# An attention and feed-forward kernel: turned tokens loaded from the host, means and deviations spread by way of DRAM

## The chip, the cores and the metric

The kernel runs on one core of one Trainium2 chip. A core has five engines with an instruction stream each: TensorE (PE in the profile; its weight loads are PEld), VectorE (DVE), ScalarE (ACT), GpSimd (POOL) and SyncE (SP), which here only issues DMAs. Engines run their own stream in order and wait for each other through semaphores. The metric is the device time of one execution in microseconds, as a median over runs.

## The reference

There are 8 sequences of 256 tokens with 256 features, all float32. Attention uses the normalized tokens as queries and the given context as both keys and values; then a gated feed-forward network with ternary weights follows, each part with a residual.

```python
def _layernorm(x, axis=-1, eps=1e-05):
    m = jnp.mean(x, axis=axis, keepdims=True)
    v = jnp.var(x, axis=axis, keepdims=True)
    return (x - m) / jnp.sqrt(v + eps)
...
        scores = jnp.einsum('bqd,bkd->bqk', query, key) * scale          # scale = 1/16
        scores = jnp.where(causal[None, :, :], neg_inf, scores)
        scores = jnp.where(key_pad, neg_inf, scores)
        attn = jax.nn.softmax(scores, axis=-1)
        out = jnp.einsum('bqk,bkd->bqd', attn, value)
...
        h = jax.nn.silu(_tlin(x, w1_w, w1_s)) * _tlin(x, w2_w, w2_s)      # 256 -> 1024
        h = jax.nn.gelu(_tlin(h, h1_w, h1_s), approximate=False)          # 1024 -> 1024
        h = jax.nn.gelu(_tlin(h, h2_w, h2_s), approximate=False)          # 1024 -> 1024
        return _tlin(h, w3_w, w3_s)                                       # 1024 -> 256
    x = x + _L0_xattn_ref(_layernorm(x, axis=-1), ctx_1024, ctx_1024, mask_BxS2_ik1)
    x = x + _L0_ffn_ref(_layernorm(x, axis=-1), ...)
```

## The kernel before

The 2048 tokens are cut into four blocks of 512 tokens (two sequences, four tiles of 128 tokens each). Attention works with tokens on the partitions, the feed-forward network with features on the partitions and the 512 tokens of a block along the free axis. So a tile of tokens has to be turned with TensorE transposes (`turned`, line 202) twice in a block before: the normalized tokens `ya` into `pqt` and from there into the queries `qt`, and the normalized tokens after attention `yf` into `pyt`, from there into the two parts `hyt` and `lyt`. The residual `xs` is turned too, into `pxt` and `xst`.

Matrix products of the feed-forward network run in a fast float32 form on a high part and a low part of the activations: ACT writes the high part, DVE subtracts it to get the low part (`rest`, line 214), and TensorE multiplies both (`layer`, line 379). Since only the weights' lower bits could make that inexact, the kernel also checks the weights: `look_through` loads pieces of the weights again into two buffers `raw` (SP, line 166), DVE reduces each to a column of `seen` (`look`, line 158), and a second, exact network, which is not run with these inputs, stands behind a branch on the outcome. Weights themselves come in by POOL's queue (line 117).

The order of work is the order in which the program is written: each engine's stream is the order of emission. `feed_forward(t)` is a generator with 26 steps: steps 0 to 7 are the gated first layer, 8 to 15 the layer `h1`, 16 to 23 the layer `h2`, 24 and 25 the output `po`. Attention for block t+1 is another generator, `stages`, and is emitted a piece at a time between the steps of block t: its pieces stand behind steps 8, 9, 11, 12, 13, 15, 17, 18, 19, 20 and 22 (`STAGES`). A load for the weight check and a look at the one before it stand behind each of the steps 8 to 20 (`LOOKS`), after the piece of attention if the step has one:

```python
            if n in STAGES:
                next(ahead, None)
            if n in LOOKS:
                next(looking, None)
```

The pieces before are, in order: statistics of `xs` (step 8), normalization to `ya` (9), the mask's bias on POOL and the transposes to `pqt` with their copies to `qt` (11), the scores `ps` and their maxima (12), exponentials (13), transposes of the probabilities (15), the product with the values and the residual (17), statistics again (18), normalization to `yf` (19), `pxt` and `xst` (20), `pyt` and its two parts (22). Block 0's attention has no earlier block to hide behind; it runs first, in two halves of one sequence each, before any feed-forward step. At the start of block t's steps the inputs of block t+1 are loaded by SP: `xs`, the mask `mi` broadcast to all partitions, the turned context `kt`, the context `vs`.

All buffers named here have one copy, except `raw`, `xst`, the hidden layers (two) and the temporary `tmp` (four), from which a step's second gelu `g` is taken.

Of the kernel before, what the change touches and what calls it, by code (L numbers as in the profile page):

```python
# [23 lines left out]
F32 = mybir.dt.float32  # L24
# [6 lines left out]
P = 128  # L31
# [28 lines left out]
def _network(ctx, tc, g, exact, flag):  # L60
# [10 lines left out]
    work = pool("work", 1)  # L71
    hp = pool("hidden", 1)
    ps_at = pool("ps_at", 4, space=bass.MemoryType.PSUM)
    ps_mm = pool("ps_mm", 4, space=bass.MemoryType.PSUM)
# [14 lines left out]
    def load_block(t):  # L89
        xs = new(io, [P, NT, D], "xs", f"xs_{t}")  # L90
        kt = new(io, [P, ND, TB], "kt", f"kt_{t}")
        vs = new(io, [P, NT, D], "vs", f"vs_{t}")
        mi = new(io, [P, TB], "mi", f"mi_{t}", I32)
        rows = bass.ts(t, TB)
        step = NT if t else 1
        for i in range(0, NT, step):
            own = bass.ds(t * TB + i * P, step * P)
            nc.sync.dma_start(  # L98
                out=xs[:, i : i + step, :], in_=g.x[own, :].rearrange("(i p) d -> p i d", p=P)
            )  # L100
        nc.sync.dma_start(out=mi, in_=g.mask[:, rows].to_broadcast([P, TB]))
        for js in groups(t):
            own = bass.ds(t * TB + js[0] * S, len(js) * S)
            nc.sync.dma_start(
                out=kt[:, :, tokens(js)],
                in_=g.ctx_t[:, own].rearrange("(c p) k -> p c k", p=P),
            )
        nc.sync.dma_start(out=vs, in_=g.ctx_n[rows, :].rearrange("(i p) d -> p i d", p=P))
        return xs, kt, vs, mi
# [29 lines left out]
    eps = new(const, [P, 1], "eps", "eps")  # L139
    nc.gpsimd.memset(eps, EPS)  # L140

    junk = new(const, [P, 1], "junk", "junk")
# [98 lines left out]

    def stages(t, js, once, result, xs, kt, vs, mi):
        cols = tokens(js)
# [5 lines left out]
        yield  # L249
        bias = once("bias", "bias", [P, NB, SW])  # L250
        for j in js:
            k0, k1 = (mi[:, j * S + k * P : j * S + (k + 1) * P] for k in range(2))
            parts = [bias[:, j, k * P : (k + 1) * P] for k in range(3)]
            nc.gpsimd.tensor_scalar(parts[1], k0, 0.0, NEG, ALU.is_equal, ALU.mult)  # L254
            nc.gpsimd.tensor_tensor(parts[0], parts[1], causal, ALU.add)
            nc.gpsimd.tensor_scalar(parts[2], k1, 0.0, NEG, ALU.is_equal, ALU.mult)
            nc.gpsimd.tensor_tensor(parts[2], parts[2], causal, ALU.add)
        qt = once("qt", "qt", [P, ND, TB])
        for n, (c, pt) in enumerate(turned(y, js, f"pqt_{t}_{js[0]}")):

            if n % 2 == 0:
                nc.scalar.activation(qt[:, c, cols], pt, AF.Copy, scale=1.0 / 16.0)
            else:
                nc.vector.tensor_scalar(qt[:, c, cols], pt, 1.0 / 16.0, None, ALU.mult)
        table(t, js, AF.Exp)
        yield
        s = once("y", "s", [P, NB, SW])
        nmax = once("nmax", "nmax", [P, NB, 2])
        for j in js:
            ps = ps_at.tile([P, TB], F32, tag="at", name=f"{v}ps_{t}_{j}")  # L270
            for h, (a, e) in enumerate(SPANS):
                for c in range(ND):
                    nc.tensor.matmul(  # L273
                        ps[:, a:e],
                        lhsT=qt[:, c, bass.ts(2 * j + h, P)],
                        rhs=kt[:, c, bass.ds(j * S, e - a)],
                        start=(c == 0),
                        stop=(c == ND - 1),
                    )
            nc.vector.tensor_tensor(s[:, j, :], ps[:, :SW], bias[:, j, :], ALU.add)  # L280
            for h, (a, e) in enumerate(SPANS):
                nc.vector.tensor_reduce(
                    nmax[:, j, h : h + 1], s[:, j, a:e], AX.X, ALU.max, negate=True
                )
# [56 lines left out]
        yield  # L341
        y = once("y", "yf", [P, NT, D])
        normed(xs, js, mvf, y, f"f_{t}_{js[0]}")
        table(t, js, AF.Silu)
        yield
        xst = once("xst", "xst", [P, ND, TB], bufs=2)
        pxt = turned(xs, js, f"pxt_{t}_{js[0]}")
        if t:
            for c, pt in pxt:
                nc.scalar.copy(xst[:, c, cols], pt)  # L350
        elif js == groups(t)[-1]:
            keep_warm(WARM_LATER)
        yield
# [3 lines left out]
        for c, pt in turned(y, js, f"pyt_{t}_{js[0]}"):  # L357
            nc.scalar.copy(yt[0][:, c, cols], pt)  # L358
            if not exact:
                rest(yt[1][:, c, cols], pt, yt[0][:, c, cols])  # L360
        if not t:
            yield
# [91 lines left out]

    STAGES = (8, 9, 11, 12, 13, 15, 17, 18, 19, 20, 22)
    LOOKS = range(NH, NH + 13)
# [79 lines left out]
```

## Time and profile before

| | us |
|---|---|
| median of 3 runs (384.49 to 386.74) | 385.27 |
| the profiled execution | 383.81 |
| its span | 381.9 |
| PE busy | 371.5 |
| ACT busy | 179.9 |
| DVE busy | 175.1 |
| POOL busy | 36.2 |

The granted TensorE clock was 0.997 over the span. Busy time counts the instructions of an engine; weight loads overlap matmuls. The lines of the profile name the line of the kernel, the engine, the operation and the tiles (out<-in, numbers left out). The chain that ended last is followed back from the last instruction, at each step to what released it, or to the instruction before it on its engine. DMA times run from issue to landing; the DMA queue of SP is called SPq. In the lists by time, a count behind an x merges neighbouring instructions, and square brackets give the idle time before and what ended it.

### The profile page before, as it was taken

The numbers are of one execution on the slowest core, as the hardware profiler recorded it, in microseconds if no ns is written. First come the engines' busy times: TensorE is split into PE (matmuls) and PEld (weight loads), VectorE is DVE, ScalarE is ACT, GpSimd is POOL, SyncE is SP. The second block draws the span as 40 slices with busy tenths as digits, with TensorE's granted clock in tenths as the row PEclk, the third lists the DMA queues.
The fourth block names the chain that finished last, engine by engine and source line by source line (L and its number), as shares of the span: only waits on it lengthen the run. The fifth ranks groups of instructions, "written<-read, shape, count | busy, mean of one in ns | idle before, by whom it ended". The sixth has DMA issues, their size and how long they took to land.

```text
span 381.9 us, 4362 instructions
## 1 busy us (share of the span) xinstructions
PE 371.5 (97%) x1660; PEld 297.8 (78%) x1661; DVE 175.1 (46%) x360; ACT 179.9 (47%) x291; POOL 36.2 (9%) x70
## 2 busy tenths in 40 slices
PE   8799999999999999999999999999999999999994
PEld 4468888888888888888888888888888888888783
DVE  4757454347226575245424755434722643322111
ACT  4466644537335562833553664443633653323320
POOL 4732260000003100000000500000000000000000
PEclk9999999999999999999999999999999999999998
DMA  6799940211008011220105303121100101110001
GB/s 194 239 399 394 383 127 30 82 57 42 13 30 247 3 56 53 57 79 32 55 0 159 118 2 108 35 80 55 49 7 37 47 0 41 30 41 0 0 2 62
DMA packets 18763, 32.87 MB, mean 86 GB/s; under 512 B 1968, under 2 KB 8880, under 8 KB 18736
## 3 DMA queue, kind: packets, MB, share of 16 engines
q1 hardware_dynamic: 14560, 20.86, 17.7%
q0 software_dynamic: 4032, 11.54, 8.6%
q8 instruction: 15, 0.25, 0.2%
q10 hardware_dynamic: 144, 0.13, 0.1%
q14 instruction: 12, 0.10, 0.1%
HBM read 30.43 MB, written 2.10 MB: 85 GB/s over the span
## 4 chain that ended last, share of the span: by engine, by line
PE 93%; DVE 1%; POOL 1%; ACT 1%; DMA 1%; SPq 0%; issue 0%
PE pm L379 63%; PE pa L379 8%; PE po L379 8%; PE pb L379 8%; PE pv L321 2%; PE ps L273 2%; DMA mi<-mask 1%; PE pxt L202 1%; PE pyt L202 1%; PE pqt L202 1%; PE pp L303 1%; SPq L98 0%; DVE xs L329 0%; DVE stf L179 0%; POOL bias L254 0%
## 5 line engine op out<-in xcount | busy, mean ns | idle before, releaser
L214 DVE TENSOR_TENSOR lh<-g,hh 128x512 fp32r<-128x512 f32 x64 | 44.5, 695 | 148.8 <-ACT g L423 148.8
L420 ACT ACTIVATE hh<-pm,sc 128x512 fp32r<-128x512 f32 x64 | 44.1, 688 | 138.2 <-PE pm L379 138.1
L379 PE MATMUL pm<-hh,h 128*128 128x512 f32 x256 | 66.3, 401 | 0.0
L379 PE MATMUL pm<-hha,h 128*128 128x512 f32 x256 | 65.7, 399 | 0.0
L379 PE MATMUL pm<-lh,h 128*128 128x512 f32 x256 | 64.9, 395 | 0.0
L379 PE MATMUL pm<-lha,h 128*128 128x512 f32 x256 | 64.9, 395 | 0.0
L379 PEld LDWEIGHTS pm<-lh,h 128*128 128x128 f32 x256 | 48.1, 188 | 11.6
L379 PEld LDWEIGHTS pm<-lha,h 128*128 128x128 f32 x256 | 48.1, 188 | 11.6
L379 PEld LDWEIGHTS pm<-hha,h 128*128 128x128 f32 x256 | 47.9, 188 | 11.2
L379 PEld LDWEIGHTS pm<-hh,h 128*128 128x128 f32 x256 | 47.4, 188 | 10.6
L423 ACT ACTIVATE g<-pm,sc 128x512 f32<-128x512 f32 x64 | 43.6, 681 | 0.0
L403 ACT ACTIVATE gate<-pa,sc 128x512 f32<-128x512 f32 x32 | 22.0, 688 | 39.2 <-PE pa L379 39.2
L406 DVE SCALAR_TENSOR_TENSOR gate<-pb,sc,gate 128x512 f32<-128x512 f32 x32 | 24.0, 750 | 21.7 <-PE pb L379 16.8
L158 DVE TENSOR_REDUCE seen<-raw 128x1 f32<-128x512 uint16 (+1 forms) x48 | 30.2, 629 | 0.0
L214 DVE TENSOR_TENSOR lha<-gate,hha 128x512 fp32r<-128x512 f32 x32 | 22.4, 699 | 0.4
L379 PE MATMUL pa<-hyt,w 128*128 128x512 f32 x64 | 20.2, 397 | 0.7 <-ACT hyt L358 0.7
L254 POOL TENSOR_SCALAR bias<-mi 128x128 f32<-128x128 int32 x8 | 6.0, 748 | 154.8 <-DMA mi<-mask 154.4
L397 ACT CAST hha<-gate 128x512 fp32r<-128x512 f32 x32 | 19.6, 611 | 2.1 <-DVE gate L406 2.1
L379 PE MATMUL pa<-lyt,w 128*128 128x512 f32 x64 | 20.2, 397 | 0.0
L379 PE MATMUL pb<-hyt,w 128*128 128x512 f32 x64 | 20.1, 396 | 0.0
L379 PE MATMUL pb<-lyt,w 128*128 128x512 f32 x64 | 20.1, 396 | 0.0
L420 ACT ACT_TABLE_LOAD x13 | 16.7, 1283 | 0.2
(78 smaller groups left out, 329.2 us busy)
## 6 DMA issues: line engine op xcount, KB each, us to landing
h<-h1t POOLq DMA_DIRECT2D x8, 512.0 KB, 10.7
h<-h2t POOLq DMA_DIRECT2D x8, 512.0 KB, 14.7
raw<-h1t SPq DMA_DIRECT2D x16, 256.0 KB, 2.6
raw<-h2t SPq DMA_DIRECT2D x16, 256.0 KB, 2.6
vs<-ctx_n SPq DMA_DIRECT2D x4, 512.0 KB, 7.0
out<-o SPq DMA_DIRECT2D x7, 256.0 KB, 2.6
xs<-x SPq DMA_DIRECT2D x3, 512.0 KB, 5.3
kt<-ctx_t SPq DMA_DIRECT2D x3, 512.0 KB, 6.4
```

The source lines that it names most:

```text
L158: nc.vector.tensor_reduce(seen[:, n : n + 1], halves16[:, :, 0], AX.X, ALU.max)
L202: nc.tensor.transpose(pt[:, c, bass.ts(n, P)], y[:, i, bass.ts(c0 + c, P)], ident)
L214: nc.vector.tensor_tensor(lo, value, hi.bitcast(F32), ALU.subtract)
L254: nc.gpsimd.tensor_scalar(parts[1], k0, 0.0, NEG, ALU.is_equal, ALU.mult)
L273: nc.tensor.matmul(ps[:, a:e], lhsT=qt[:, c, bass.ts(2 * j + h, P)], rhs=kt[:, c, bass.ds(j * S, e - a)], start=(c == 0), stop=(c == ND - 1),)
L321: nc.tensor.matmul(pv[:, h, :], lhsT=prt[:, j, bass.ds(a + k * P, P)], rhs=vs[:, 2 * j + k, :], start=(k == 0), stop=(k == n - 1),)
L379: nc.tensor.matmul(pm, lhsT=wc[:, bass.ts(o, P)], rhs=x, start=(n == 0), stop=(n == len(steps) - 1),)
L397: nc.scalar.copy(hid[0][:, o, :], value)
L403: nc.scalar.activation(gate, pa, AF.Silu, scale=sc[:, 0, o : o + 1])
L406: nc.vector.scalar_tensor_tensor(values[o], pb, sc[:, 1, o : o + 1], gate, ALU.mult, ALU.mult)
L420: nc.scalar.activation(nxt[0][:, o, :], pm, AF.Gelu, scale=scale)
L423: nc.scalar.activation(value, pm, AF.Gelu, scale=scale)
```

## The change

For the blocks 1 to 3, the queries and the input of the feed-forward network are no longer turned on TensorE.

- The host passes a further array, `xt`, the turned tokens. `queries_loaded` loads a block of it into `qt`. The statistics are computed as before; the means go to all partitions through DRAM (`on_all`: a write of four values per partition, then a read that broadcasts the row of 512), DVE subtracts the row from `qt`, and the factor one over sixteen times the deviation is applied later, to the scores (`factor`, in one operation with the bias).
- For the feed-forward network, mean and reciprocal deviation both go through DRAM (two writes, two broadcast reads). `xst`, which is still turned on TensorE, less the mean (DVE) times the reciprocal deviation (POOL) gives `yf` in turned form. The two parts are taken from it a step later, behind step 23, which is new in `STAGES`.
- The rows land in a new tile `row` and, for the reciprocal deviations, in the mask's tile `mi`.
- In block 0 the four compare operations of the mask move from POOL to DVE; the additions stay on POOL.
- The space for POOL's DMA descriptors is set to 8192 bytes.

```diff
+    rows = pool("rows", 2, space=bass.MemoryType.DRAM)
...
-    def stages(t, js, once, result, xs, kt, vs, mi):
+    def mask_bias(t, js, once, mi):
+        bias = once("bias", "bias", [P, NB, SW])
+        engine = nc.gpsimd if t else nc.vector
+        for j in js:
+            k0, k1 = (mi[:, j * S + k * P : j * S + (k + 1) * P] for k in range(2))
+            parts = [bias[:, j, k * P : (k + 1) * P] for k in range(3)]
+            engine.tensor_scalar(parts[1], k0, 0.0, NEG, ALU.is_equal, ALU.mult)
+            nc.gpsimd.tensor_tensor(parts[0], parts[1], causal, ALU.add)
+            engine.tensor_scalar(parts[2], k1, 0.0, NEG, ALU.is_equal, ALU.mult)
+            nc.gpsimd.tensor_tensor(parts[2], parts[2], causal, ALU.add)
+        return bias
+
+    def on_all(values, tags, name):
+
+        n = values.shape[2]
+        there = new(rows, [n, NT, P], f"{len(tags)}", f"{name}")
+        for i in range(n):
+            nc.sync.dma_start(out=there[i].rearrange("i p -> p i"), in_=values[:, :, i])
+        got = []
+        for i, (p, tag, dt) in enumerate(tags):
+            row = new(p, [P, TB], tag, f"{name}{i}", dt).bitcast(F32)
+            nc.sync.dma_start(
+                out=row, in_=there[i : i + 1].rearrange("o i p -> o (i p)").to_broadcast([P, TB])
+            )
+            got.append(row)
+        return got
...
+    def queries_loaded(t, js, once, xs, mi):
+        qt = once("qt", "qt", [P, ND, TB])
+        nc.sync.dma_start(
+            out=qt, in_=g.xt[:, bass.ts(t, TB)].rearrange("(c p) q -> p c q", p=P)
+        )
+        mva = once("mva", "mva", [P, NT, nc.vector.BN_AGGR_DIM])
+        sums(xs, js, mva, f"a_{t}")
+        (mean,) = on_all(mva[:, :, 0:1], ((work, "row", F32),), f"ma_{t}")
+        yield
+        bias = mask_bias(t, js, once, mi)
+
+        std = once("sq", "sda", [P, NT])
+        nc.scalar.activation(std, mva[:, :, 1], AF.Sqrt, bias=eps256, scale=256.0)
+        rstd = once("rstd16", "rstd", [P, NT])
+        nc.vector.reciprocal(rstd, std)
+        yield
+        for c in range(ND):
+            nc.vector.tensor_tensor(qt[:, c, :], qt[:, c, :], mean, ALU.subtract)
+        yield
+        return qt, bias, rstd
...
-            nc.vector.tensor_tensor(s[:, j, :], ps[:, :SW], bias[:, j, :], ALU.add)
+            if factor is None:
+                nc.vector.tensor_tensor(s[:, j, :], ps[:, :SW], bias[:, j, :], ALU.add)
+            else:
+                for h, (a, e) in enumerate(SPANS):
+                    nc.vector.scalar_tensor_tensor(
+                        s[:, j, a:e],
+                        ps[:, a:e],
+                        factor[:, 2 * j + h : 2 * j + h + 1],
+                        bias[:, j, a:e],
+                        ALU.mult,
+                        ALU.add,
+                    )
...
+        if t:
+            std = once("sq", "sdf", [P, NT])
+            nc.scalar.activation(std, mvf[:, :, 1], AF.Sqrt, bias=eps)
+            nc.vector.reciprocal(mvf[:, :, 1], std)
+            mean, rstd = on_all(mvf, ((work, "row", F32), (io, "mi", I32)), f"mf_{t}")
+            yield
+            for c, pt in turned(xs, js, f"pxt_{t}"):
+                nc.scalar.copy(xst[:, c, :], pt)
+            yield
+            y = once("y", "yf", [P, ND, TB])
+            for c in range(ND):
+                nc.vector.tensor_tensor(y[:, c, :], xst[:, c, :], mean, ALU.subtract)
+                nc.gpsimd.tensor_tensor(y[:, c, :], y[:, c, :], rstd, ALU.mult)
+            yield
+            for c in range(ND):
+                nc.scalar.copy(yt[0][:, c, :], y[:, c, :])
+                if not exact:
+                    rest(yt[1][:, c, :], y[:, c, :], yt[0][:, c, :])
...
-    STAGES = (8, 9, 11, 12, 13, 15, 17, 18, 19, 20, 22)
+    STAGES = (8, 9, 11, 12, 13, 15, 17, 18, 19, 20, 22, 23)
...
+        "xt": turned(given["x"].reshape(B * S, D)),
...
-    nc = bacc.Bacc("TRN2", target_bir_lowering=False, num_devices=1)
+    nc = bacc.Bacc("TRN2", target_bir_lowering=False, num_devices=1, dynamic_dma_scratch_size=8192)
```

More of the change, by code (lines that the diff above doesn't have):

```diff
@@ L93, in load_block @@
         mi = new(io, [P, TB], "mi", f"mi_{t}", I32)
-        rows = bass.ts(t, TB)
+        span = bass.ts(t, TB)
         step = NT if t else 1
@@ L100, in load_block @@
             )
-        nc.sync.dma_start(out=mi, in_=g.mask[:, rows].to_broadcast([P, TB]))
+        nc.sync.dma_start(out=mi, in_=g.mask[:, span].to_broadcast([P, TB]))
         for js in groups(t):
@@ L107, in load_block @@
             )
-        nc.sync.dma_start(out=vs, in_=g.ctx_n[rows, :].rearrange("(i p) d -> p i d", p=P))
+        nc.sync.dma_start(out=vs, in_=g.ctx_n[span, :].rearrange("(i p) d -> p i d", p=P))
         return xs, kt, vs, mi
@@ L140, in _network @@
     nc.gpsimd.memset(eps, EPS)
+    eps256 = new(const, [P, 1], "eps256", "eps256")
+    nc.gpsimd.memset(eps256, 256.0 * EPS)
     junk = new(const, [P, 1], "junk", "junk")
@@ L240, in table, with queries_turned @@
             nc.scalar.activation(junk, eps, func)
-    def stages(t, js, once, result, xs, kt, vs, mi):
+    def mask_bias(t, js, once, mi):
[22 more added lines that the diff above has]
+        return got
+    def queries_turned(t, js, once, xs, mi):
         cols = tokens(js)
@@ L249, in stages @@
         yield
[L250 to L257, printed above, removed]
-        qt = once("qt", "qt", [P, ND, TB])
[L259 to L264, printed above, removed]
+        bias = mask_bias(t, js, once, mi)
+        qt = once("qt", "qt", [P, ND, TB])
+        for c, pt in turned(y, js, f"pqt_{t}_{js[0]}"):
+            nc.scalar.activation(qt[:, c, cols], pt, AF.Copy, scale=1.0 / 16.0)
         table(t, js, AF.Exp)
         yield
+        return qt, bias, None
+    def queries_loaded(t, js, once, xs, mi):
[7 more added lines that the diff above has]
+        yield
+        bias = mask_bias(t, js, once, mi)
+        std = once("sq", "sda", [P, NT])
[7 more added lines that the diff above has]
+        return qt, bias, rstd
+    def stages(t, js, once, result, xs, kt, vs, mi):
+        cols = tokens(js)
+        queries = queries_loaded if t else queries_turned
+        qt, bias, factor = yield from queries(t, js, once, xs, mi)
         s = once("y", "s", [P, NB, SW])
@@ L341, in stages @@
         yield
[L342 to L345, printed above, removed]
         xst = once("xst", "xst", [P, ND, TB], bufs=2)
[L347 to L353, printed above, removed]
         yt = [once("yth", "hyt", [P, ND, TB], dt=FR)]
@@ L356, in stages @@
             yt.append(once("ytl", "lyt", [P, ND, TB], dt=FR))
[L357 to L361, printed above, removed]
+        if t:
[16 more added lines that the diff above has]
+                    rest(yt[1][:, c, :], y[:, c, :], yt[0][:, c, :])
+        else:
+            y = once("y", "yf", [P, NT, D])
+            normed(xs, js, mvf, y, f"f_{t}_{js[0]}")
+            table(t, js, AF.Silu)
+            yield
+            pxt = turned(xs, js, f"pxt_{t}_{js[0]}")
+            if js == groups(t)[-1]:
+                keep_warm(WARM_LATER)
+            yield
+            for c, pt in turned(y, js, f"pyt_{t}_{js[0]}"):
+                nc.scalar.copy(yt[0][:, c, cols], pt)
+                if not exact:
+                    rest(yt[1][:, c, cols], pt, yt[0][:, c, cols])
             yield
```

## The prediction

> **What bounds the kernel now.** I read first the page's busy times and the chain that ended last, then the chain piece by piece, then DVE, PE and SP in order of time around the steps that the change touches, last the table of DMA issues.
>
> ```profile
> PE 371.5 (97%) x1660; PEld 297.8 (78%) x1661; DVE 175.1 (46%) x360; ACT 179.9 (47%) x291; POOL 36.2 (9%) x70
> ...
> PE 93%; DVE 1%; POOL 1%; ACT 1%; DMA 1%; SPq 0%; issue 0%
> ```
>
> The chain piece by piece (start us, us, what), the start and the third later block:
>
> ```profile
> 2.58 3.68 DMA mi<-mask
> ...
> 6.34 0.65 POOL bias L254
> ...
> 10.82 0.46 POOL bias L257
> ...
> 11.31 0.57 DVE s L280
> ...
> 233.35 0.87 PE pqt L202 x8
> 234.22 3.73 PE pm L379 x16
> 237.96 2.62 PE ps L273 x16
> ...
> 282.00 0.87 PE pyt L202 x8
> ```
>
> From 21.77 to 376.5 us the chain is TensorE without a gap, so any matmul or transpose taken out there is worth its time, and any wait put in there costs its time. Before 21.77 it is a chain of small steps through the mask, and POOL is on it from 6.34 to 11.29. In order of time (start us, us, engine, line):
>
> ```profile
> 5.99 0.79 DVE L189 TENSOR_SCALAR ya<-xs,mva,rsa 128x256 f32<-128x256 f32 x2
> ...
> 7.46 2.86 PE L273 MATMUL ps<-kt,qt 128*128 128x128 f32 x16
> ...
> 9.11 0.56 DVE L280 TENSOR_TENSOR s<-ps,bias 128x384 f32<-128x384 f32 x1 [2.34 <-PE ps L273]
> ...
> 11.31 0.56 DVE L280 TENSOR_TENSOR s<-ps,bias 128x384 f32<-128x384 f32 x1 [0.99 <-POOL bias L257]
> ```
>
> In a later block the weight checks (`raw`) are loaded by SP one step ahead of DVE's look at them (SP in order of time):
>
> ```profile
> 207.09 25.97 SPq L166 DMA_DIRECT2D raw<-h2t  x4
> ```
>
> The first of these four was issued at 207.1, some 20 us before DVE's look needs it: SP has nothing ahead of it that waits. That is the cover which the change takes. SP's queue and DMA issues (KB each, us from issue to landing):
>
> ```profile
> q1 hardware_dynamic: 14560, 20.86, 17.7%
> ...
> raw<-h2t SPq DMA_DIRECT2D x16, 256.0 KB, 2.6
> ...
> xs<-x SPq DMA_DIRECT2D x3, 512.0 KB, 5.3
> ...
> raw<-w3t SPq DMA_DIRECT2D x8, 128.0 KB, 2.0
> ...
> out<-o SPq DMA_DIRECT2D x1, 128.0 KB, 2.6
> ...
> sc<-scales SPq DMA_DIRECT2D x1, 16.0 KB, 5.2
> s<-w3s SPq DMA_DIRECT2D x1, 1.0 KB, 4.8
> ```
>
> The first of these lines is SP's queue (packets, MB, share of 16 engines' span): 20.86 MB in 17.7% of 16 x 381.9 us is 19 GB/s for one DMA engine, 53 ns for 1 KB. The last two were issued at 4.55 and 5.10, so they landed 0.15 us apart.
>
> **Part 1, transposes gone.** Each later block loses 8 of `pqt` and 8 of `pyt`. Both groups stand on the chain with 0.87 us each; 3 blocks x 2 x 0.87 = 5.22 us less.
>
> **Part 2, block 0's mask on DVE.** Four of POOL's eight mask operations go to DVE. The mask lands at 6.3, DVE is free at 6.78 (end of `ya`). A 128x128 operation costs DVE 0.29 us (its maximum of that size, 286 ns); the first is ready at 7.07, and POOL's four additions (0.46 plus 0.07 between) run to about 9.2. Late next is PE: the second `ps` ends at 7.46 + 2.86 = 10.32. So the second `s` starts at 10.36 instead of 11.31: 0.95 us less, carried to the end because everything behind it to 21.77 hangs on it. The weight loads behind POOL's mask start 2 us earlier, which hurts nothing I can see.
>
> **Part 3, the mean by way of DRAM.** At step 8 of the earlier block SP gets, ahead of that step's weight check: the load of `qt` (issued early, at about 207.5, no wait), the write of four means per partition (waits for DVE's statistics), the broadcast read (waits for the write), and only then the check's load. Behind it on DVE stand, in order: the look at that check (step 9), the rest of step 10, a look, the rest of step 11, then the two subtractions that give `qt`. TensorE's next stop is `ps`.
>
> In the times of the third later block: the last statistic ends at 227.95. With W for the write from issue to landing, the read is issued at 228.05 + W. The check behind it lands 3.95 later: 2.0 fixed (the smallest landing, `raw<-w3t`), 1.3 for 256 KB of broadcast at the 200 GB/s that the traffic fell to while `mi` was moving, 0.65 for its own 256 KB at 390 GB/s. That is 232.0 + W. From there DVE needs four operations at 0.61 apart, one subtraction 0.61, one 0.69: 3.7 us, to 235.7 + W. TensorE, without the transposes, wants the second half of `qt` at 237.73 - 0.87 = 236.86 (weight loads of `ps` begin at 237.57 before). So TensorE stands still for S = W - 1.1.
>
> W is in no row: 512 runs of 4 bytes into DRAM, 32 on each DMA engine. From below, 2.0, the smallest landing of any size. From above, 5.3, `xs`, which is also 512 runs, of 1 KB. Nearest by direction is the 128 KB write, 2.6, of which 8 packets an engine at 53 ns are 0.4: 2.2 fixed. The 32 runs add between 0.6 (`s`, 8 runs of 8 bytes on each engine, landed 0.15 after `sc`: 19 ns each) and 1.7 (at 53 ns). I take the middle, W = 3.3, and S = 2.2; ends 0.9 and 4.2, and 0 if the broadcast moves at full rate as well. Three blocks: 6.6. In the first later block weights still move at 330 to 390 GB/s until 48 us, just when the write goes out: 0.4 more, bounds 0 and 2.
>
> A rule speaks against it: the Trainium skill, "DMA: Bandwidth & Descriptors", section "Rules for kernel authors", says that a last dimension with a stride becomes one descriptor per element and should be rearranged to be contiguous. Its section "Bandwidth" gives a floor of about 10.5 ns per packet over all engines; an estimate by that page is 512 x 10.5 = 5.4 us on top of 2.2, W = 7.6, S = 6.5, and the whole change 14 us slower. The trace's 8-byte runs are reads into SBUF; no row here shows such writes.
>
> **Part 4, the feed-forward's mean and deviation.** At step 19 two writes and two reads go to SP, and a check's load behind them. The reciprocal ends at 273.07; the first read goes out at 273.15 + W, and the check lands 5.25 later (2.0 fixed, two broadcasts, its own 0.65), at 278.4 + W = 281.7, where DVE's look stood at 276.1. DVE waits 5.6 us, but behind it stands only the rest of step 21 (nominal 279.6), needed by `po` at 290: hidden. Then at step 22: two subtractions from 284.0 to 285.3, POOL's two multiplications of 128x512, each between 0.70 (DVE's time for it) and 1.84 (four times POOL's 0.46 for 128x128); by 1.84 they end at 288.4, ACT's copy at 289.0, DVE's rest at 289.7. The next `pa` starts at 293.92 - 0.87 = 293.05: 3.3 us of cover. Cost nothing, and up to 3 us a block if the writes take 5 each.
>
> **Part 5, the rest.** The scaling inside `s` splits one DVE operation into two (0.55 to about 0.8): DVE sits idle 2.8 us before it. The scalings of `y` and `qt`'s copies leave DVE and ACT, which are not the bound. Seven more DMAs a block at 0.45 us on SP, 3.75 MB in all against 32.9: beside the work, save for parts 3 and 4. The smaller scratch for POOL's DMAs: POOL's waits before are for the eighth load ahead of it to land, so I cost it at nothing; were it the limit, weights come later than the 2 us they gain, with h1 needed only at 36.
>
> **Sum.** -5.22 - 0.95 + 6.6 + 0.4 = +0.8 us. The profiled execution took 383.81 (span 381.9), 1.46 under the median of 385.27; it would take 384.6, and the median 386.1.
>
> **Rivals.** A: the round trip fits. The mean needs only to be there at 235.3, and if the write lands in 2.3 us or less and the broadcast is quick, S falls to 0 to 1.2. For it: the smallest landings of 2.0; against: TensorE's margin counts the check's load too. All gone: 385.27 - 6.2 + 0.4 = 379.5; with S = 1.2, 383.1. B, slower: the 4-byte writes are what decides. From W = 3.7 (S = 2.6) the three stalls outweigh both gains by over 0.5%; at 5.3 it is 385.27 - 5.8 + 12.6 = 392.1. For it: 32 runs an engine and writes that share lines of DRAM; against: the 8-byte runs at 19 ns. C: POOL's multiplications come late at the block's end and `pa` waits; it decides once the chain is 3.3 us longer than worked out; with 2 us a block, 392.1. Against: it takes more than four times POOL's time for a quarter of the tile.
>
> **How the numbers follow.** About 0.5% (1.9 us) is what a measurement can tell from no change. The forecast's mechanism with W of 2.8 to 4.0, own range 384.6 to 388.2: 0.50, of which 0.37 within the bound and 0.13 slower. A 0.22 (0.20 faster, 0.02 same), B 0.23 (slower), C 0.05 (0.04 slower, 0.01 same). Faster 0.20, same 0.40, slower 0.40. Range 381.0 to 391.5: it leaves out the part of A below S = 0.6 (0.1) and the parts of B and C past W = 5.1 (0.1).
>
> **What would show it.** PE loses 48 transposes and its count falls by as many; the second `s` of block 0 starts at 10.4. In each later block PE shows an idle stretch of 2 us ahead of `ps`, put down to DVE's subtraction, and DVE a wait ahead of the look at `raw` put down to its DMA; SP waits for `ma`. `pa` starts without a gap behind `po`. I am wrong if `ps` starts on time, if the wait ahead of the subtraction is for the mean itself and not for the look, or if a gap shows elsewhere: before `pa`, or in the first layer for want of weights.

## The result and the profile after

The change costs 38 us: the median is 423.8 us (422.0 to 426.74, 6 runs) against 385.41 of the kernel before on the same chip (384.49 to 386.74, 6 runs), a ratio of 1.0998 (95% interval 1.0954 to 1.1042). The forecast was 386.1 with a range up to 391.5. The profiled execution took 422.0 us, its span is 420.2, and its mean granted TensorE clock 0.955, where it was 0.997 before.

The page of the kernel after, first the busy times, then the granted clock in 40 slices of the span, then the shares of the chain that ended last:

```profile
PE 377.9 (90%) x1613; PEld 299.5 (71%) x1613; DVE 178.6 (42%) x355; ACT 179.3 (43%) x288; POOL 43.0 (10%) x73
...
PEclk9999977999989998699999999689999999999998
...
PE 65%; DMA 19%; DVE 8%; ACT 3%; issue 3%; SPq 1%; DVEq 0%
```

The instructions of TensorE fall from 1660 to 1613 (48 transposes are gone; one matmul of the kernel before has no record), but its busy time rises by 6.4 us, and its idle time, the span less the busy time, from 10.4 to 42.3 us. So 31.9 of the 38.3 us of longer span are standing still, and 6.4 are the same or less work done more slowly. The chain, which was TensorE's alone, now runs through DMAs for a fifth of its length. The sevens and sixes in the clock's row say when.

Chain of the kernel after, in the third later block (start us, us, what), from the last statistic to the scores:

```profile
253.52 8.48 DMA ma<-mva
...
262.02 0.34 SPq L266
...
262.41 6.01 DMA raw<-h2t
...
268.44 0.69 DVE seen L161
...
270.92 0.61 DVE qt L309
...
271.58 5.60 PE ps L323 x16
```

The write of four means a partition, 2 KB in all, takes 8.48 us. SP cannot issue the broadcast read before it has landed, and the weight check `raw` is loaded behind that read. DVE stands before its look at the check, and the subtraction that makes `qt` stands behind the look. VectorE in order of time, the same place, shows the wait in brackets:

```profile
268.44 0.69 DVE L161 TENSOR_REDUCE seen<-raw 128x1 f32<-128x512 uint16 x1 [13.69 <-DMA raw<-h2t]
...
270.84 1.28 DVE L309 TENSOR_TENSOR qt<-qt,ma 128x512 f32<-128x512 f32 x2
```

That is the queue that the prediction laid out, look, rest, look, rest and two subtractions, with the wait in front of the look. The stretches of the same span (start and end, length, busy time of PE, PEld, DVE, ACT and POOL with their counts, then granted clock, share of the DMA engines, GB/s) add two things:

```profile
253.00:262.00 9.00, 9.00 (x40) 7.22 (x39) 1.72 (x5) 5.16 (x7) 0.00 (x0) 1.00 0.03 0
262.00:268.00 6.00, 0.63 (x3) 0.19 (x1) 0.00 (x0) 1.27 (x2) 0.00 (x0) 0.90 0.41 109
268.00:271.60 3.60, 0.02 (x1) 0.02 (x1) 3.15 (x6) 0.00 (x0) 0.00 (x0) 0.50 0.37 125
```

While the write is under way the DMA engines are busy for 3% of the time: almost nothing is being moved, so the time does not go into moving bytes. And 4.1 us after TensorE has stopped, at 262.6, its granted clock falls to 0.50 (2.9 and 4.5 us after the stop in the first and second later block), so that `ps` takes 5.60 us where it took 2.62. The Trainium skill, "TensorE: Matmul & The Clock Gate", section "HAM oscillation — how this bites in real kernels", says that gaps above about 3.4 us throttle the array again. The gaps of 8 to 9 us here do so in all three blocks; and a shorter one can, too, as the output layer shows below.

TensorE's waits in the kernel after (total us, times, longest):

```profile
PE ps L323 <- DVE qt L309: 17.5, 2, 8.9
PE ps L323 <- issue: 8.1, 1, 8.1
PE po L455 <- DVE lh L217: 6.1, 3, 2.4
```

The first two lines are the three later blocks ahead of their scores, 25.6 us together. The third is new as well: three times the products `po` of the output layer stop for a low part `lh`. The chain of the kernel after in the feed-forward part of the third later block says why:

```profile
309.72 8.83 DMA mf<-mvf
...
318.99 5.62 DMA raw<-h2t
...
324.63 0.69 DVE seen L161
...
326.52 1.20 DVE yf L418 x2
327.72 1.68 DVE lh L217
...
329.44 2.60 PE po L455 x10
```

It is the same write, the same queue, and this time the rest `lh` of the layer before stands behind the check and the two subtractions. That rest is slow besides; it runs beside POOL's two multiplications:

```profile
327.35 3.19 POOL L419 TENSOR_TENSOR yf<-yf,mf 128x512 f32<-128x512 f32 x2 [85.21 <-PE po L455]
327.64 1.75 DVE L217 TENSOR_TENSOR lh<-g,hh 128x512 fp32r<-128x512 f32 x1
```

Away from POOL's work the same operation takes 0.69 us. It takes 1.75 at this place in all three later blocks, so 1.06 us of each stop of 1.8 to 2.4 come from here. No run takes the multiplications away and leaves the rest as it is; that they are the reason is read from the coincidence alone.

In the first later block this stop lasts 2.37 us, and the stretches of a microsecond around it (columns as above) show the clock falling within the second microsecond after it and at one half from 124 on:

```profile
120.00:121.00 1.00, 0.00 (x0) 0.00 (x0) 1.00 (x2) 0.00 (x0) 1.00 (x1) 1.00 0.00 0
...
124.00:125.00 1.00, 1.00 (x3) 0.73 (x3) 1.00 (x2) 1.00 (x1) 0.00 (x0) 0.50 0.00 0
```

The stops of the other two blocks, 1.78 and 1.95 us, leave the clock as it is. So 2.4 us can be enough here, less than the page has it, but the length alone does not decide. In the four profiles with these slow writes ahead of `po` (this one and three of the runs below) there are ten stops of 2.37 or 2.38 us: the half clock came with seven of them and not with three. It also came behind a stop of 2.08 us ahead of `ps` (the run with useless matmuls), and not behind one of 2.29 (the run with long writes).

The DMA issues of the kernel after (KB each, median us from issue to landing):

```profile
ma<-ma SPq DMA_DIRECT2D x3, 256.0 KB, 5.2
...
mf<-mvf SPq DMA_DIRECT2D x6, 2.0 KB, 8.7
ma<-mva SPq DMA_DIRECT2D x3, 2.0 KB, 8.5
```

The balance, all from rows of the two profiles: transposes -5.22; the start-up -0.25 (the first `pa` at 21.52 instead of 21.77); waits ahead of `ps` +25.6; `ps` itself 21.9 us busy instead of 13.1, +8.8; waits ahead of `po` +6.1; `po` of the low part 18.2 busy instead of 16.2, +2.0; `pa` 41.2 instead of 40.4, +0.8. The sum is +37.8, the span grew by 38.3. The last two terms are rough, since busy times of overlapping matmuls count twice: by its starts, the work behind the stop of the first later block came 1.6 us late. The -0.25 is no more than scatter: in the two runs with small writes below, whose start-up is that of the kernel before, the first `pa` stands at 21.82 and 24.02.

### The profile page after: what moved, and what is told of

It reads as the page before. It is cut to its first block, busy times and chain, and to the rows that moved or that the text cites. A ratio compares the mean times of both kernels' runs of the same rounds, so it can differ in the third digit from the quotient of the medians.

```text
span 420.2 us, 4303 instructions
## 1 busy us (share of the span) xinstructions
PE 377.9 (90%) x1613; PEld 299.5 (71%) x1613; DVE 178.6 (42%) x355; ACT 179.3 (43%) x288; POOL 43.0 (10%) x73
## 4 chain that ended last, share of the span: by engine, by line
PE 65%; DMA 19%; DVE 8%; ACT 3%; issue 3%; SPq 1%; DVEq 0%
PE pm L455 39%; PE pa L455 7%; PE pb L455 7%; DMA mf<-mvf 7%; PE ps L323 5%; DMA raw<-h2t 4%; DMA ma<-mva 4%; PE po L455 4%; DVE lh L217 3%; DMA raw<-h1t 3%; PE pv L382 2%; DMA kt<-ctx_t 1%; DVE seen L161 1%; DVE yf L418 1%; ACT hh L496 1%
## 5 line engine op out<-in xcount | busy, mean ns | idle before, releaser
L217 DVE TENSOR_TENSOR lh<-g,hh 128x512 fp32r<-128x512 f32 x64 | 47.0, 738 | 113.9 <-ACT g L499 113.9
L455 PEld LDWEIGHTS pm<-lha,h 128*128 128x128 f32 x256 | 48.0, 187 | 11.8
L455 PEld LDWEIGHTS pm<-lh,h 128*128 128x128 f32 x256 | 48.0, 187 | 11.8
L323 PE MATMUL ps<-kt,qt 128*128 128x128 f32 (+1 forms) x64 | 19.5, 489 | 26.0 <-DVE qt L309 17.5
L323 PEld LDWEIGHTS ps<-kt,qt 128*128 128x128 f32 x64 | 15.2, 294 | 29.5 <-DVE qt L309 18.3
L419 POOL TENSOR_TENSOR yf<-yf,mf 128x512 f32<-128x512 f32 x6 | 9.6, 1612 | 240.2 <-PE po L455 171.5
L455 PE MATMUL po<-lh,w 128*128 128x512 f32 x64 | 18.2, 419 | 6.1 <-DVE lh L217 6.1
```

What stands on the lines that cost most here:

```text
L217: nc.vector.tensor_tensor(lo, value, hi.bitcast(F32), ALU.subtract)
L323: nc.tensor.matmul(ps[:, a:e], lhsT=qt[:, c, bass.ts(2 * j + h, P)], rhs=kt[:, c, bass.ds(j * S, e - a)], start=(c == 0), stop=(c == ND - 1),)
L419: nc.gpsimd.tensor_tensor(y[:, c, :], y[:, c, :], rstd, ALU.mult)
L455: nc.tensor.matmul(pm, lhsT=wc[:, bass.ts(o, P)], rhs=x, start=(n == 0), stop=(n == len(steps) - 1),)
```

## Experiments

Times are medians; ratios are to the kernel before on the same chip, with a 95% interval. Three medians of the kernel before belong to the groups of runs: 384.89 (7 runs), 385.71 (11 runs) and 385.39 (7 runs).

### What is slow about the write

Six small DMAs were put into the last block of the kernel before, a few steps apart in the program, where nothing waits for them: the change's own write (`runs`: 512 runs of 4 bytes), 128 runs of 4 bytes (`few`), of 32 (`long`) and of 128 (`wide`), 512 of 4 bytes from SBUF to SBUF (`inner`), and 512 of 4 bytes that lie 64 bytes apart in DRAM (`apart`). Times of the kernel say nothing here, the landings do.

```diff
+        if n == 1:
+            nc.sync.dma_start(
+                out=dram("runs", [NT, P]).rearrange("i p -> p i"), in_=vals[:, :, 0]
+            )
+        if n == 7:
+            nc.sync.dma_start(
+                out=dram("few", [1, P]).rearrange("i p -> p i"), in_=vals[:, 0:1, 0]
+            )
+        if n == 10:
+            nc.sync.dma_start(
+                out=dram("long", [P, 2 * NT]), in_=vals.rearrange("p i s -> p (i s)")
+            )
...
+            nc.sync.dma_start(
+                out=dram("apart", [P, NT, 16])[:, :, 0], in_=vals[:, :, 0]
+            )
```

> The kernel before, with small writes added on SP's queue beside the last block's feed-forward steps, 7 to 11 us apart, that nothing waits for: 512 runs of 4 bytes into DRAM as in the change (runs), 128 of 4 bytes (few), 128 of 32 bytes (long), 128 of 128 bytes (wide), 512 of 4 bytes of which each has a 64-byte line of DRAM for itself (apart), and 512 of 4 bytes from SBUF to SBUF (inner). If the number of runs sets the time: runs and apart 8.5 us, few, long and wide 3 to 4, inner well under runs only if DRAM costs more per run. If a short write into DRAM takes long whatever the number: runs, few, long and apart all near 8.5, inner 2 to 3. If it is runs that share a line: runs and few slow, long, apart and inner 2.5 to 3.5. One read that broadcasts a row written 20 us earlier (rowold): 3.3 if it was the fresh write that made the reads of the change slow, 5.2 if such a read is slow by itself. The whole kernel stays within 0.5% of before.

DMA issues of this kernel (KB, us from issue to landing):

```profile
runs<-vals SPq DMA_DIRECT2D x1, 2.0 KB, 11.1
few<-vals SPq DMA_DIRECT2D x1, 0.5 KB, 10.8
long<-vals SPq DMA_DIRECT2D x1, 4.0 KB, 1.9
inner<-vals SPq DMA_DIRECT2D x1, 2.0 KB, 3.6
...
apart<-vals SPq DMA_DIRECT2D x1, 2.0 KB, 2.7
```

512 runs of 4 bytes are quick when they lie 64 bytes apart (`apart`, 2.7) or go to SBUF (`inner`, 3.6). Runs of 128 bytes (`wide`) took 1.8. So neither the number of runs nor their shortness makes the 8 to 11 us. But `few` had been issued 0.4 us behind `runs` and may only have stood in its wake, and `runs` differs from `apart` in two things, the distance and that its neighbours in DRAM come from different partitions. A second set took `few` by itself, four 4-byte runs of one partition side by side (`near`), 16 bytes a partition (`quad`), and 4-byte runs 32 bytes apart in two orders (`step`, `line`). Each landing was seen once.

```diff
+            nc.sync.dma_start(out=dram("near", [P, NT]), in_=vals[:, :, 0])
...
+            nc.sync.dma_start(
+                out=dram("quad", [P, NT]), in_=vals[:, 0:2, :].rearrange("p i s -> p (i s)")
+            )
...
+            nc.sync.dma_start(out=dram("step", [P, NT, 8])[:, :, 0], in_=vals[:, :, 0])
...
+            nc.sync.dma_start(
+                out=dram("line", [NT, P, 8])[:, :, 0].rearrange("i p -> p i"), in_=vals[:, :, 0]
+            )
```

> The kernel before with further small writes that nothing waits for, each released by DVE a step or more after the last, so that none is queued behind another: 128 runs of 4 bytes into one stretch (few); 512 runs of 4 bytes where a partition's four lie side by side (near); 128 of 16 bytes (quad); 512 of 4 bytes, each 32 bytes from the next, in the same order (step), and in the change's order (line); 128 of 32 bytes (long), and a read that broadcasts 2 KB of it 3.7 us later (rownew). The first probes told that neither the number of runs nor their being short makes them slow (512 apart by 64 bytes took 2.7 us). If several runs in one line of DRAM are slow however they come: few, near and quad 6 to 11, step, line and long 2 to 3. If it takes neighbours from different DMA engines: near 3 to 4, because four side by side come from one engine. If few was only slow because it stood behind the other slow write: few 2 to 3. If reads of freshly written rows are slow: rownew 5, otherwise 3.5.

DMA issues of the kernel with the second set:

```profile
few<-vals SPq DMA_DIRECT2D x1, 0.5 KB, 7.9
near<-vals SPq DMA_DIRECT2D x1, 2.0 KB, 8.2
quad<-vals SPq DMA_DIRECT2D x1, 2.0 KB, 1.4
...
line<-vals SPq DMA_DIRECT2D x1, 2.0 KB, 2.3
```

`few` is as slow by itself, with 128 runs. `near` is slow although a run's neighbours come, but for the ends of each four, from its own partition; so it does not take a different partition on every side. Whether partitions that meet every 16 bytes matter is not separated. `line` is the change's own order with 32 bytes from run to run, and quick (`step`, the same in the order of partitions, took 3.6); `quad` has the bytes of `near` back to back in runs of 16, and is quick. What is slow is 4-byte runs that lie side by side in DRAM. The runs show this as a pattern; what in the memory or the DMA engines makes it so, they do not show. It also puts aside the estimate that the prediction made by a page, at W = 7.6: that is near the 8.5 measured by luck, since it counts packets, and 512 runs of 4 bytes land in 2.3 when they are 32 bytes apart. Two reads that broadcast 2 KB of such a row were put in as well: `rowold`, issued 23 us behind the write of 4-byte runs, landed in 3.5, `rownew`, issued as soon as a row of 32-byte runs had landed, in 3.3. Why the change's own reads took 5.2 is open; other loads follow them on the queue at once.

### Each part alone

One kernel has the change for the queries only, with the feed-forward part as before; the other the reverse.

```diff
+        y = once("y", "yf", [P, NT, D])
+        normed(xs, js, mvf, y, f"f_{t}_{js[0]}")
...
-            mean, rstd = on_all(mvf, ((work, "row", F32), (io, "mi", I32)), f"mf_{t}")
```

```diff
-        queries = queries_loaded if t else queries_turned
+        queries = queries_turned
```

> Only the queries come from the loaded layout, with the mean by way of DRAM; the feed-forward input is turned on TensorE as before. If the loss sits ahead of the scores (idle 9 us a block while the mean and the checks behind it come in, and 3 us more because the clock is low after it): 385.4 + 3 x 12 - 2.6 = 419 us. If the feed-forward half carries as much: about 404.

Measured: 418.78 (417.34 to 419.61), ratio 1.0865 (1.0824 to 1.0906).

> Only the feed-forward input takes mean and deviation by way of DRAM; the queries are turned on TensorE as before. If this half costs only the 2 us wait inside po in each block: 385.4 + 6.1 - 2.6 = 389 us. If the halves weigh the same: about 404. If it is hidden, as my prediction had it: 382.8.

Measured: 390.88 (389.69 to 391.67), ratio 1.0142 (1.0109 to 1.0176). TensorE's waits, first with the queries' part alone ("issue" is a wait for nothing that the profile shows; the look at `raw` ahead of it on DVE waits 14 us for its DMA in each of the three blocks), then with the feed-forward part alone:

```profile
PE ps L323 <- issue: 29.4, 3, 10.5
```

```profile
PE po L455 <- DVE lh L217: 7.1, 3, 2.4
```

So the queries' part carries 34 of the 38 us, with the waits ahead of `ps` and none ahead of `po`; the feed-forward part makes the waits ahead of `po`. The second part's price is flattered, though: in that kernel the matmuls `pm` follow each other at 227 ns, in the kernel before and the changed one at 233. That is worth about 6.6 us (the kernel before gains as much by it, below) and has nothing to do with turned tokens; the last section of experiments finds out what it is. Without it the feed-forward part alone would stand at about 397.5, 13 us above the kernel before. That 34 and 13 are more than 38 is to be seen in the rows: alone, the waits ahead of `ps` are 29.4 instead of 25.6, those ahead of `po` 7.1 instead of 6.1, and `po` of the low part is busy for 22.8 us instead of 18.2, since the clock falls in all three blocks. These are 9.4 us together.

### The clock

Is the slow `ps` a matter of the clock? In this kernel, 38 matmuls whose result nobody reads are put ahead of `ps` in each later block, so that TensorE is busy while it waits; all else is the changed kernel.

```diff
+    FILL = 38
+    def fill(times):
+        warm = ps_at.tile([P, TB], F32, tag="at", name="fill")
+        for _ in range(times):
+            nc.tensor.matmul(warm, lhsT=w1[0][:, :P], rhs=w1[0][:, :TB], start=True, stop=True)
...
         yield
+        fill(FILL)
         return qt, bias, rstd
```

> The changed kernel with 38 matmuls of no use ahead of the scores of each later block, about as long as TensorE's idle stretch there. If the slow scores (5.6 us against 2.6 before) come from the granted clock falling while TensorE stands still: the scores take 2.6 again, the clock stays at 1.0, and the time falls by 9 to 415 us. If they are slow for another reason (the operands, a port): scores 5.6 and 424 us.

Measured: 424.81 (424.38 to 425.05), ratio 1.1034 (1.1001 to 1.1067): not faster. TensorE in order of time at the scores of the third later block, behind 8.80 us of useless matmuls:

```profile
275.38 3.27 PE L333 MATMUL ps<-kt,qt 128*128 128x128 f32 x16 [0.84 <-DVE qt L318]
```

`ps` takes 3.27 us for all 16 and 2.66 for its last 14, and the granted clock stays at 1.00 there, so it was the clock. Why is it not in the total? From the end of `pm` to the end of `ps` this block takes 12.7 us against 14.5 in the changed kernel: `ps` is 2.3 shorter and begins 0.5 later. The second later block gains as much. But in the first, the write landed 11.8 us after its issue instead of 9.1, TensorE stopped for 2.08 us behind the useless matmuls, the clock fell to 0.50 again and `ps` there still took 4.94; its end is 2.75 us later than in the changed kernel. And ahead of `po` TensorE now stops for 2.37 us in each block instead of 2.37, 1.78 and 1.95, with the slow clock behind two of the stops instead of one. The distance of the two profiled executions goes 2.75 (end of the first `ps`), 3.1 and 1.7 (first and second `po`), 1.5 (end of the third `ps`), 2.1 (third `po`), 2.7 at the end. The slow clock is thus shown as the reason for the slow `ps`, and a gain of 1.8 us a block with it; that all of the 8.8 us would come back without it is not shown, since the landings of the writes moved by more than was gained.

### The write made long

Means and deviations of a partition, eight values side by side, go out as one run of 32 bytes, and the whole row of 4 KB comes back to all partitions; DVE and POOL then read every second value of it, in the order of partitions.

```diff
-            nc.sync.dma_start(out=there[i].rearrange("i p -> p i"), in_=values[:, :, i])
+        there = new(rows, [P, NT * 2], "stats", f"{name}")
+        nc.sync.dma_start(out=there, in_=values.rearrange("p i s -> p (i s)"))
+        row = new(work, [P, P * NT * 2], "row", f"{name}0")
...
+        got = row.rearrange("q (p i s) -> q s i p", i=NT, s=2)
...
-            nc.vector.tensor_tensor(qt[:, c, :], qt[:, c, :], mean, ALU.subtract)
+            nc.vector.tensor_tensor(by_tile(qt[:, c, :]), by_tile(qt[:, c, :]), mean, ALU.subtract)
```

> The changed kernel with means and deviations written as one run of 32 bytes a partition (both values of all four tiles), read back as a row of 4 KB to all partitions; DVE and POOL read it with a step. If the slow write is what costs the time: the write lands in 2 to 3 us, the wait ahead of po goes, and 2 us of wait ahead of the scores stay in each block because the read and the check behind it still take 7 us: 385 - 5 + 7 = 387 us, up to 391 if the clock falls in that wait. If it is the way through DRAM and the queue as such: 410 or more.

Measured: 388.01 (384.96 to 391.31, 8 runs, a wider scatter than the others'), ratio 1.0051 (1.0013 to 1.0089). Two of TensorE's waits, and of the DMA issues the write:

```profile
PE ps L323 <- DVE qt L309: 3.4, 5, 1.1
PE ps L323 <- issue: 2.3, 1, 2.3
```

```profile
ma<-mva SPq DMA_DIRECT2D x3, 4.0 KB, 1.4
```

One layout gives back 36 of the 38 us, though the read is twice as large. The wait ahead of `po` is gone, the clock is at 0.992, and 5.7 us of waiting ahead of `ps` are left in three blocks. The prediction's formula would leave 0.3 a block for a write of 1.4; but the read of 512 KB lands 4.2 us after its issue, and the two subtractions with a stride take 2.1 us instead of 1.3. In the profiled execution the start-up is late, too: the first `pa` comes at 24.09 instead of 21.77, behind a context `kt` for which TensorE waits 1.6 us.

### The statistics early

The other way out is time: the changed kernel, its slow writes included, with the next block's statistics at step 4 in place of step 8.

```diff
-    STAGES = (8, 9, 11, 12, 13, 15, 17, 18, 19, 20, 22, 23)
+    STAGES = (4, 9, 11, 12, 13, 15, 17, 18, 19, 20, 22, 23)
```

> The changed kernel with the statistics for the queries, and with them their way through DRAM, behind step 4 in place of step 8; the writes stay as slow as they are. If the wait ahead of the scores is lateness alone: it goes, with the low clock behind it, and only the feed-forward half is left: 424 - 36 = 388 us, 2.6 less than with that half alone. If the slow write hurts by other means too (traffic, SP): above 395.

Measured: 399.34 (399.04 to 399.56), ratio 1.0355 (1.0328 to 1.0382), 11 more than expected. Two of TensorE's waits:

```profile
PE po L455 <- DVE lh L217: 7.7, 4, 2.4
PE ps L323 <- issue: 6.3, 1, 6.3
```

The second and third later blocks start their scores on time, as expected. The first waits 6.3 us and has its `ps` at the slow clock (4.96 us). SP in order of time has its write and the read that waits for it 19 us apart:

```profile
34.72 0.37 SPq L262 DMA_DIRECT2D ma<-mva  x1
...
53.76 0.34 SPq L266 DMA_DIRECT2D ma<-ma  x1
```

Up to 45 us weights come in at 350 to 400 GB/s. How much of the 19 us is their doing, the next kernel shows.

The rest of the miss is a wrong start of the sum: the expectation took the feed-forward part's price from the kernel that had it alone, with its faster `pm`. From rows like those of the balance (transposes, the wait and the slow `ps` of the first block, the waits ahead of `po` and the slow `po` behind one of them), 385.7 - 5.2 + 6.3 + 2.3 + 7.7 + 2 = 398.8.

### Both, and the pace of the matmuls

With long writes and early statistics together nothing should wait. Besides, I wanted to know what made `pm` faster in one of the kernels. Where the tiles lie in SBUF differs between the kernels: in the kernel before and in the changed one the weights and the activations `hha`, `hh`, `lh` that they multiply start 32 bytes apart modulo 64, in the kernel with the feed-forward part alone at the same place. (These places are reckoned from the sizes of the tiles in the order of the program, each rounded up to 32 bytes; the traces show no addresses.) Padding of 32 bytes a partition tests it: once in the kernel before ahead of the hidden layers, once in the kernel before ahead of all working tiles (so that `hyt` and `lyt` agree with the weights too), and once in the repaired kernel. In this order:

```diff
+    new(hp, [P, 8], "pad", "pad")
```

```diff
+    new(work, [P, 8], "pad", "pad")
```

```diff
+    new(io, [P, 8], "pad", "pad")
```

> The kernel before with 32 bytes put ahead of the hidden layers in SBUF, nothing else. In the run with the feed-forward half alone the matmuls of h1, h2 and po followed each other every 227 ns, in all others every 233; there the weights and the hidden layers start at the same place within 64 bytes, in the others 32 apart. If that is the reason: 227 ns here too, 1152 x 6.5 ns = 7.5 us less, 377.4; pa and pb stay at 232.5. If not: 384.9.

> The change with both repairs: each partition's means and deviations go out as one 32-byte run (128 of them) and a 4 KB row comes back to every partition, and the statistics of the next block are taken at step 4 of the feed-forward in place of step 8. If the time lost was the late write and what queued behind it, no later block waits ahead of its scores or of the first product of its feed-forward, the granted clock stays above 0.99, and what is left is the gain on the chain: 385.4 - 5.2 = 380.2, up to 2 more where the context lands late in the start-up as it did in the run with long rows alone: 380 to 383. If the first later block still waits because of the weights that are loading then, as it did for 6.3 us with the early statistics and the slow write, 386 to 388. If the elementwise work with a stride (2.0 us for a pair of subtractions in place of 1.2) or the spread row's 512 KB reads hold something up, a wait on DVE of 1 to 2 us a block ahead of the scores, 384 to 387.

> The kernel before, with 32 bytes of padding ahead of the working tiles, so that hidden layers and normalized activations start at 0 of 64 as the weights do (in the earlier run with padding only the hidden layers did, and pm alone went faster). If agreement is the cause, pa and pb go faster too, at about 228 ns against 236.7 and 232.5: 379.15 - 1.3 = 377.8 (376.5 to 378.8). It tells what of the time of the last version is the alignment, and what the change.

> The kernel of the run before with 32 bytes of padding on each partition ahead of the working tiles, so that normalized activations, hidden layers and weights all start at the same place within 64 bytes (32 of 64; in the run with padding in the kernel before it was 0 for weights and hidden layers). If it is the agreement of weights and activations that counts, the 1152 products of the feed-forward's pm go at 227 to 228 ns instead of 233.5 and pa and pb follow to about 228: the time falls by 6.7 + 1.3 = 8 against the run before, to about 372.5 (371 to 375 with a start-up late by up to 2). If it is the place itself that counts (0 of 64), pm stays at 233.5 and the time at that of the run before.

| kernel | us (range) | ratio (interval) |
|---|---|---|
| before, hidden layers padded | 379.15 (378.92 to 379.82) | 0.9834 (0.9806 to 0.9861) |
| before, all padded | 376.14 (375.68 to 376.67) | 0.9762 (0.9735 to 0.9788) |
| long writes, early statistics | 381.07 (380.25 to 381.45) | 0.9887 (0.9859 to 0.9914) |
| the same, padded | 374.94 (374.60 to 375.29) | 0.9738 (0.9712 to 0.9763) |

The page of the kernel with long writes and early statistics:

```profile
PE 367.7 (97%) x1613; PEld 292.9 (77%) x1613; DVE 184.9 (49%) x355; ACT 179.6 (47%) x288; POOL 45.9 (12%) x73
...
PEclk9999999999999999999999999999999999999998
```

TensorE has 3.8 us less to do than in the kernel before and its clock is never lower; no wait of TensorE ahead of `ps` is over 1.0 us, and none is left ahead of `po`. So with both repairs the change is worth 4.3 us, near the 5.2 of the transposes. In the two profiled executions 2.5 of it stand behind the first `pa`: from there to the end it takes 357.7 us instead of 360.2.

One write is late even here. The first later block's, now one run of 32 bytes a partition, goes out while the weights come in, and SP issues the read behind it 12.0 us later:

```profile
35.34 0.34 SPq L260 DMA_DIRECT2D ma<-mva  x1
...
47.38 0.34 SPq L262 DMA_DIRECT2D ma<-ma  x1
```

So long runs alone do not make a write quick: this one took 12.0 us in traffic of 360 to 400 GB/s (11.9 in the padded kernel below), where the others took 1.4. Of the 19 us of the early statistics with slow writes, an estimate from this is that 12 are the weights' share and 7 the layout's. Here the early issue hides it.

The groups of matmuls by line (busy us, mean ns), the kernel before and the kernel before with all tiles padded:

```profile
L379 PE MATMUL pm<-lh,h 128*128 128x512 f32 x256 | 64.9, 395 | 0.0
...
L379 PE MATMUL pa<-lyt,w 128*128 128x512 f32 x64 | 20.2, 397 | 0.0
```

```profile
L381 PE MATMUL pm<-lh,h 128*128 128x512 f32 x256 | 63.3, 389 | 0.0
...
L381 PE MATMUL pa<-lyt,w 128*128 128x512 f32 x64 | 19.8, 391 | 0.0
```

With only the hidden layers padded, `pm` has the second kernel's 389 and `pa` the first one's 397: each follows its own operands. From start to start `pm` goes from 233.3 to 227.1 ns on the mean, `pa` and `pb` from 233.3 to 226.8. It is agreement and not the place itself: 0 of 64 for both, or 32 of 64 for both, is faster than 0 and 32. The repaired kernel, at 32 and 32, is a little slower than the others (`pm` at 229.1 from start to start), which is why it came out at 374.94 and not at the 372.5 expected; I don't know why. The padded kernel before did better than expected by 1.7 us: `pa` and `pb` gained 256 times 6.5 ns, 1.7 us, and not the 1.3 I had put down; the rest of the difference is open.

Set side by side, both padded, the change with its repairs stands at 374.94 and the kernel before at 376.14. The ranges do not overlap; the change is worth 1.2 us there, where it was worth 4.3 without padding. But the profiled executions put this 1.2 into the start-up: the first `pa` stands at 23.50 in the padded kernel before and at 21.76 in the padded repaired one, and from there to the end they take 351.4 and 351.1 us. The start-up scatters that much from one execution to the next (21.77 to 24.02 in the kernel before and its two copies with small writes). So that the change is still worth anything behind the start-up, once both are padded, is not shown. Of the 3.1 us between 4.3 and 1.2, 1.5 are `pm` (257.2 us busy against 255.7); the rest is open.

## Why the prediction was wrong

**The step that failed is W, in part 3.** The mechanism was right in each piece: the read waits for the write, the check's load stands behind the read, DVE's look waits for the check, the subtractions stand behind the look, TensorE behind them. The size of its one unknown was not: taken at 3.3, with an upper end of 5.3, it measured 8.5 to 11.3 in the changed kernel. I had built the upper end from a load of 512 runs, and the chosen value from reads of 8 bytes into SBUF. Neither writes to DRAM, and neither has 4-byte runs side by side; the fixed cost that I took for a write, 2.2, came from one with long runs. Rows of another direction and another layout were no bound at all. With 8.5 in the prediction's own formula S is 7.4; measured is 8.1 to 8.9, because read and check landed together 14.9 us after the last statistic and not 12.6.

**Rival B was the true one,** and its reason, writes that share lines of DRAM, was on the right track in that runs side by side are the slow ones; its price stopped at 5.3, and its 32 runs an engine are not the cause. It had 0.23. The argument against it, the 8-byte runs at 19 ns, was about reads.

**The clock was left out.** No step of the prediction had TensorE slow down after a stall, since the kernel before never stalls long enough to show it. Behind the stops of 8 to 9 us it adds 2.9 us to each `ps`, and behind one of the short ones ahead of `po` 1.6 to the matmuls that follow; a stop of 2.08 us was enough once, so even with the forecast's S of 2.2 the step would have needed it as a possible cost.

**Part 4 fell with the same W.** The chain was named rightly, down to DVE's wait (11.85 us where 5.6 were worked out with W = 3.3; the check landed 14.9 us after the reciprocal, and W + 5.3 gives 14.2). Hidden it was only up to the rest that `po` needs; past that point it costs 2 us a block. I had looked for the loss at `pa` (rival C). It came earlier: the rest that `po` needs stands behind the subtractions and runs beside POOL's multiplications, and there it took 1.75 us in place of 0.69, a cost that the prediction put at nothing. POOL's two multiplications took 3.19 us, within the 1.84 each that were allowed.

**Part 2** measured 0.25 instead of 0.95, and even that is within the scatter of the start-up. The second scores of block 0 came at 11.06, not at 10.4: the mask was no longer late, but the context `kt` landed 4.91 us after its issue, `ps` began at 8.09 instead of 7.46, and took the place of the mask. I had named PE as the next that is late, and had not asked what PE waits for.

**Part 1 and part 5 held.** The 48 transposes went, worth 5.2 on the chain, and nothing showed of the cheaper items.

## What to carry to other kernels

A round trip through DRAM is priced by its layout: give each partition's values a run of 16 or 32 bytes, or leave 32 bytes between single values, and have the reader undo it. Layout alone does not help against traffic: beside the weights' loads a long write was late as well. When a chain of waits hangs on one duration that no row shows, a range from unlike rows isn't a range; put the operation where its lateness hurts least, and keep loads that others wait for from standing behind it in the same queue. And a stall of TensorE costs more than its length once the clock falls.

## What the runs showed of the hardware

- Writes to DRAM of 4-byte runs side by side landed 7.9 to 11.8 us after issue whether there were 128 or 512 of them, and 19 us when issued into the weight loads; 512 runs of 4 bytes 32 or 64 bytes apart landed in 2.3 to 3.6, runs of 16, 32 and 128 bytes in 1.4 to 1.9, but 12.0 for runs of 32 bytes issued into the weight loads. The DMA engines were busy for 3% of one of the slow writes.
- A 128x512 subtraction of VectorE took 1.75 us beside GpSimd's multiplications of the same size, and 0.69 away from them.
- The granted clock of TensorE fell to 0.50 after 2.9 to 4.5 us of the long stops, and also with stops of 2.08 and 2.37 us, though not with every one of that length.
- The same matmuls with 512 columns went at 227 to 229 ns from start to start where weights and activations started, as reckoned, at the same place modulo 64 bytes in SBUF, and at 233 where they were 32 bytes apart. In the kernel before this is worth 9.3 us, 2.4%, for 32 bytes of padding: more than the 5.2 us of all the transposes that the change removes.
